# Two-layer cross-attention on one core: the last third of the even entries' queries one filling point later, and layer 2's image-key copy on ScalarE in place of GpSimd

## The chip, the cores and the metric

The kernel runs on one core of a Trainium2 chip. TensorE (PE) multiplies matrices into the eight banks of PSUM. VectorE (DVE), ScalarE (ACT) and GpSimd (POOL) do the elementwise work, and SyncE (SP) issues nearly all DMA transfers. Each engine works through its own instructions in order and waits on semaphores for the others. The metric is the device time of one execution in microseconds (us), and the time of a kernel is the median of its runs.

## The reference

Sixteen entries (B) of 256 rows and 320 channels pass through two cross-attention layers with 20 heads of 16 channels. The context of an entry has 256 rows of 512 channels. In layer 1 its first 77 rows (`T0`) are text and the others image tokens; in layer 2 the first 252 (`T1`) are text and the last 4 image tokens. Layer 1 in short:

```python
q = hidden_states @ Wq
k_text, v_text = text @ Wk, text @ Wv
probs = softmax(q_h @ k_h.T * scale)                 # per head, over the text
text_out = probs @ v_h
scores = q_h @ ip_k_h.T * scale                      # ip_k = ip @ Wk_ip
sem = (softmax(q @ k_text.T * scale) @ text) @ ip.T * scale
ip_probs = softmax(scores + 0.5 * sem) * spatial_mask
hs = text_out + ip_probs @ ip_v_h
out = hs @ Wout + bout + residual
```

Layer 2 does the same on layer 1's output with its own weights, but takes the semantic term per head, from that head's own text probabilities, and with both sides scaled to length one:

```python
qsem = l2norm(probs_t @ text_ehs)                    # per head
sem = qsem @ l2norm(ip_ehs).T
probs_ip = softmax(q @ k_ip.T * scale + 0.5 * sem) * spatial_mask
```

## The kernel before

**Slots.** The work is cut into 160 slots: 80 for layer 1, 16 entries by 5 groups of four heads, and then 80 for layer 2. In slot k of layer 1 (`slot0`), PE transposes the row maxima of slot k+1 (`maxima0`, line 708), computes scores for slot k+2 (`score0`, 701), multiplies for the exponentials of slot k (`turned0`, 723) and multiplies the probabilities of slot k-1 by the values (`attend0`, line 766). ACT copies the transposed maxima out of PSUM (line 710, tile `mt`) and issues their transfer into the query tiles `qs` (711); it also takes the exponentials (726). POOL multiplies them by the semantic factors (729), and DVE takes the row maxima (702, 703). Slots of layer 2 (`slot1`) have the exponentials at line 879, the maxima's transpose at 884, copy at 886 and transfer at 887, and the semantic products on all engines (894 rounds the probabilities on ACT, 895 takes the remainder on POOL, 904 multiplies on PE, 905 multiplies on DVE).

**Filling.** Between those steps, at three points of each slot, `fill(now)` runs whatever other work is due: keys, queries, values, semantics, the closing projections. Each such task is a generator with a list of due times in slots. PE's instructions stand in the order in which the code issues them. Those of the other four engines are ordered by a scheduler, so an edit of one task may move instructions on them too.

**Queries.** `queries0(b)` loads an entry's rows (`xq`), splits them in a high and a low half (`hq`) and projects in three pieces: two of eight matmuls (line 567) and a third of five (line 570, m = 2). The third is emptied by `evacuate` in four steps: ACT copies at 266 (`q`) and 267 (`both`), DVE works at 268 and 269, and then SP writes the third piece to DRAM (`qd<-q`), from where the slots' tiles `qs` are loaded four slots ahead. The output projection of an earlier entry (`close0`) uses the same two lines with the split rows `ho`, which ACT makes at 554 and 555 and POOL at 556 and 557. All these products share the rotating PSUM banks named `X`.

**Keys of layer 2.** `keys1(b)` does the same for the keys, in three pieces with the two buffers `kst` in turn. The last four columns of each piece (`T1:`) are the image tokens' keys, which were computed for all entries at once in `kip`. Line 490 copies them into `kst`, high and low part at once, and `keys_out` writes `kst` to DRAM (`kd<-kst`, two transfers per piece, at line 84). The copy must wait until the transfers of the piece that used that buffer before have read it.

Of the kernel before, what the change touches and what calls it, by code (L numbers as in the profile page):

```python
# [26 lines left out]
T1 = S - NIP  # L27
# [23 lines left out]
def xattn2(  # L51
# [27 lines left out]
    nc = tc.nc  # L79
    f = lambda ap: ap.bitcast(F32)  # L80
# [10 lines left out]
    def bank(tag="X"):  # L91
        return ps.tile([128, 512], F32, tag=tag, name=tag, bufs=BANKS[tag])
# [18 lines left out]
    def buf(tag, shape, dtype=F32, bufs=1, name=None):  # L111
        if tag in ("wB", "wD", "vr", "raw"):
            return sb.tile(shape, dtype, tag=tag, name=name or tag, bufs=bufs)
        size = 1
        for d in shape[1:]:
            size *= d
        if tag not in slots:
            slots[tag] = [0, dtype] + [const_tile([128, max(size, words.get(tag, 0))], f"{tag}_{i}", dtype) for i in range(bufs)]
        n, kind, *ring = slots[tag]
        assert kind == dtype and len(ring) == bufs, tag  # L120
        slots[tag][0] += 1
        t = ring[n % bufs][: shape[0], :size]
        names = "abcd"[: len(shape) - 1]
        if len(names) > 1:
            t = t.rearrange(f"p ({' '.join(names)}) -> p {' '.join(names)}", **dict(zip(names, shape[1:])))
        return t

    def const_tile(shape, tag, dtype=F32):
        return const.tile(shape, dtype, tag=tag, name=tag)
# [121 lines left out]
    def prod_m(out, w, m, rhs, kt):  # L251

        if m < 2:
            prod(out, lambda s, k: w(s, k, m), rhs, kt)
            return out
        for i in range(2 * kt):
            mm(out, w(0, i // 2, 2), rhs(i % 2, i // 2), start=i == 0, stop=i == 2 * kt - 1)  # L257
        return out

    def evacuate(hi, lo, out, m):  # L260

        if m < 2:
            return halves(hi, lo, out)
        hi, lo = hi[:64], lo[:64]
        both = buf("both", list(hi.shape), bufs=2)
        nc.scalar.copy(hi, out[:64])
        nc.scalar.copy(both, out[64:])
        nc.vector.tensor_sub(out[:64], out[:64], f(hi))
        nc.vector.tensor_add(lo, out[:64], both)  # L269

    def context(b, n, wait=0):

        tiles, parts = [], []
        for k in range(0, 4, 3 - n):
            src = cT_d[:, b * S : (b + n) * S].rearrange("(k p) t -> p k t", p=128)[:, k : k + 3 - n]
            ct = buf("cta" if n == 1 or k < 2 else "ctb", [128, 2, 512], FR, bufs=SIZES["CTA" if n == 1 or k < 2 else "CTB"], name="ct")
            split = lambda t: t.rearrange("p (k t) -> p k t", t=n * S)
            parts.append((src, split(ct[:, 0]), split(ct[:, 1])))
            tiles.append(ct)
        yield from in_turn(parts, wait, "rawc raw" if n == 2 else "rawc", nc.gpsimd if wait and b != 2 else nc.vector)  # L280
        if n == 2:
            return lambda s, k: tiles[k][:, s].rearrange("p (b t) -> p b t", b=2)
        return lambda s, k: tiles[k // 2][:, s, (k % 2) * S : (k % 2 + 1) * S]
# [25 lines left out]
    kip = const_tile([128, 2, 3, BI], "kip", FR)  # L309


    def keys_out(d, m, kst, b=slice(None)):

        rows = slice(m * 128, min(m * 128 + 128, CH))
        n = rows.stop - rows.start
        for r, s in ((slice(0, 2), 0), (slice(2, 3), 1)):
            src = kst[:n, s, b].rearrange("p b t -> p (b t)").unsqueeze(1)
            dma(d[r, rows, b].rearrange("r p b t -> p r (b t)"), src.to_broadcast([n, r.stop - r.start, src.shape[2]]))
# [163 lines left out]
    def keys1(b):  # L482
        ct = ct1[b] = yield from context(b, 1, 0.3)
        for m in range(3):
            kst = buf("kst", [128, 2, 2, S], FR, bufs=SIZES["KST"]).rearrange("p s b t -> p (s b t)")
            kst = kst[:, : 2 * S].rearrange("p (s b t) -> p s b t", s=2, b=1)
            kp = prod_m(bank()[:, :T1], w1["k"], m, lambda s, k: ct(s, k)[:, :T1], 4)
            n = 64 if m == 2 else 128
            evacuate(kst[:, 0, 0, :T1], kst[:, 1, 0, :T1], kp, m)
            nc.gpsimd.tensor_copy(kst[:n, :, 0, T1:], f(kip[:n, :, m, 4 * b : 4 * b + 4]))  # L490
            keys_out(kd[1][b], m, kst)
            if m < 2:
                yield
        wv = w1["wv"]
        two = [buf("tph", [128, 2, S], FR, bufs=2, name="two") for i in range(2)]
        twice = doubled[b] = lambda k: two[k // 2][:, k % 2, :T1]
        for k in range(4):
            nc.gpsimd.tensor_copy(wv[:, :, k, H * D :], f(ct(slice(None), k)[:, :, T1:]))
        for k in range(4):
            nc.scalar.activation(twice(k), f(ct(1, k)[:, :T1]), AF.Copy, scale=2.0)  # L500
        yield
# [48 lines left out]
    def split(src, neg, eng, tag):  # L550

        hl = buf(tag, [128, 5, S], FR)
        order = queued if tag == "hq" else lambda inst: inst
        order(nc.scalar.copy(hl[:, 0:2], src[:, 0:2]))
        order(nc.scalar.activation(hl[:, 2], src[:, 2], AF.Copy, scale=neg))
        order(eng.tensor_sub(hl[:, 3:5], src[:, 0:2], f(hl[:, 0:2])))
        order(eng.tensor_add(hl[:, 2], src[:, 2], f(hl[:, 2])))
        return hl
# [15 lines left out]
    def queries(l, a):  # L574
        qh = buf("q", [128, 2, 3, S], FR)

        def evac(m, pp):
            evacuate(qh[:, 0, m], qh[:, 1, m], pp, m)

        qd = dram.tile([3, CH, S], F32, tag=f"qd{l}", name=f"qd{l}", bufs=2)  # L580
        steps = project(l, wq[l], a, evac)
        for m in range(2):
            next(steps)
            yield
        for r, s in ((0, 0), (1, 1), (2, 0)):
            dma(qd[r, :256].rearrange("(m p) t -> p m t", p=128), qh[:, s, :2])
        next(steps)
        for r, s in ((slice(0, 3, 2), 0), (slice(1, 2), 1)):
            to = qd[r, 256:].rearrange("r p t -> p r t")
            dma(to, qh[:64, s, 2].unsqueeze(1).to_broadcast(list(to.shape)))  # L590
        yield
        return qh, qd
# [4 lines left out]
    def load(src, tag):  # L597
        x = buf(tag, [128, 3, S])
        dma(x, src.rearrange("(k p) t -> p k t", p=128))
        return x  # L600

    def queries0(b):
        x = early.pop(b) if b in early else load(xT_d[b], "xq")
        yield
        xs = split(x, tmask[:, 5:6], nc.gpsimd, "hq")
        yield
        return (yield from queries(0, xs))
# [662 lines left out]
    def task(key, times, make, *needs):  # L1270
        tasks[key] = [times, 0, make, needs, len(tasks)]
# [38 lines left out]
    def shifted(n, *times):  # L1310

        return [RAMP(n + t) for t in times]
# [4 lines left out]
    for c in range(B // 2):  # L1317
        n, k = 10 * c, [("k0", c)] if c else []
        if c:
            task(("k0", c), FIRST["k0"] if c == 1 else shifted(n, -14.4, -13.3, -13, -12.4, -12, -11.4, -10.8, -9.8, -9.4, -9, -8.4), lambda c=c: keys0(c),  # L1320
                 *([("w4", 0)] if c > 1 else []))
            task(("q0", 2 * c), shifted(n, -11.8, -11, -10, -9, -8), lambda b=2 * c: queries0(b))
        task(("q0", 2 * c + 1), shifted(n, -4.4, -4, -3, -2.8, -2), lambda b=2 * c + 1: queries0(b))
        if c:
            task(("m0t", 2 * c), shifted(n, -7.4), lambda b=2 * c: tokens0(b), *k)
        task(("m0t", 2 * c + 1), shifted(n, -4.8), lambda b=2 * c + 1: tokens0(b), *k)
        task(("v0", 2 * c), shifted(n, -7, -5.4, -5), lambda b=2 * c: values0_(b), *k)
        task(("v0", 2 * c + 1), shifted(n, -4, -3.8, -3.4), lambda b=2 * c + 1: values0_(b), *k)
        for b, t in ((2 * c, (-7.4, -6.4, -6, -5.4, -5, -4.4, -3.4)), (2 * c + 1, (-2.4, -1.8, -1.4, -1, -0.8, 0, 1.2))):
            if b:  # L1330
                task(("s0", b), FIRST["s0"] if b == 1 else shifted(n, *t), lambda b=b: semantic0(b), ("q0", b), ("m0t", b))
            task(("c0", b), shifted(5 * b, *((6, 7.6, 8, 8.2) if b % 2 == 0 else (6, 7.2, 8.2, 9.2) if b < B - 1 else (7, 7.67, 8, 8.67))), lambda b=b: close0(b), ("gathered", 0, b), ("w4", 0))
    for b in range(B):
        n = NS + 5 * b
# [340 lines left out]
```

## Time and profile before

| | |
|---|---|
| median of 3 runs | 1478.3 us (1476.85 to 1479.2) |
| profiled execution | 1483.24 us |
| its span on the core | 1481.5 us |
| mean granted clock of PE | 0.983 |
| busy: PE, POOL, DVE, ACT | 1418.0, 1217.7, 1133.5, 897.5 us |
| line 490 on POOL | 48 copies, 192 ns each in the middle |

The profile is one execution, in microseconds from the start of its span. A row of the timeline gives the start, the length, the engine, the line and the operation with its tiles, and in brackets how long the engine had stood idle before it and what released it. A row of the table of waits gives the total, the number and the longest. Layer 1's slots run to about 640 us and layer 2's from about 690, where an entry of five slots takes 48.9 us.

### The profile page before, as it was taken

Reading aid. Unit: us, or ns where it says so; the run is one execution under the profiler, and the core shown is the slowest. Engines: PE = TensorE matmul, PEld = TensorE weight load, DVE = VectorE, ACT = ScalarE, POOL = GpSimd, SP = SyncE. Lnnn points to the kernel's source line nnn. Section 1 sums busy time; section 2 is a strip of 40 time slices with the busy share of each in tenths; the row PEclk is TensorE's granted clock in tenths of the full one; section 3 lists DMA queues with packets and bytes.
Section 4 is the critical chain, followed back from the end, with each engine's and each line's share of the span. In section 5 each row is a group of like instructions: output and inputs, shape, how many; then the busy total and the mean of one; then the engine's idle time right before and its main releaser. Section 6 shows DMA issues by size and latency. Waiting matters only on the chain.

```text
span 1481.5 us, 35836 instructions
## 1 busy us (share of the span) xinstructions
PE 1418.0 (96%) x12578; PEld 1147.1 (77%) x12578; DVE 1133.5 (77%) x2527; ACT 897.5 (61%) x2173; POOL 1217.7 (82%) x1590
## 2 busy tenths in 40 slices
PE   8889999999999989789999999999999999999998
PEld 7778888888888878567778777877787777777765
DVE  6567777777777788867878888788878878887886
ACT  6346565656565645546666676666766766676663
POOL 6259898989999978889678888788878888888885
PEclk8899999999999999989999999999999999999999
DMA  7766777776777665765444444444444444533401
GB/s 241 199 205 202 214 209 214 204 213 193 229 205 219 201 202 160 198 201 157 138 105 124 126 135 110 125 140 120 116 119 138 121 116 120 147 114 93 125 25 51
DMA packets 229118, 232.43 MB, mean 157 GB/s; under 512 B 38186, under 2 KB 198860, under 8 KB 228940
## 3 DMA queue, kind: packets, MB, share of 16 engines
q1 hardware_dynamic: 226736, 229.18, 54.2%
q8 instruction: 100, 1.64, 0.5%
q10 hardware_dynamic: 2204, 0.97, 0.3%
q14 instruction: 78, 0.64, 0.1%
HBM read 117.65 MB, written 77.07 MB: 131 GB/s over the span
## 4 chain that ended last, share of the span: by engine, by line
PE 69%; POOL 10%; DVE 9%; DMA 4%; ACT 3%; issue 3%; SPq 1%; ACTq 0%; DVEq 0%; POOLq 0%
PE X L904 14%; PE X L247 14%; PE P L766 6%; PE X L567 6%; PE S L701 5%; PE P L916 4%; PE P L926 4%; PE T L723 4%; POOL wt L895 3%; PE T L859 3%; PE S L865 3%; POOL P L729 3%; PE X L257 2%; DMA qs<-qd 2%; PE X L570 1%
## 5 line engine op out<-in xcount | busy, mean ns | idle before, releaser
L729 POOL TENSOR_TENSOR P<-P,rs 128x512 f32<-128x512 f32 x320 | 408.1, 1304 | 80.4 <-ACT P L726 79.7
L895 POOL TENSOR_TENSOR wt<-P,ctb 128x512 f32<-128x512 f32 x316 | 402.4, 1293 | 39.8 <-ACT ctb L894 39.3
L904 PE MATMUL X<-ctb,gm 128*128 128x512 f32 x1106 | 295.4, 400 | 4.5 <-DVE wt L905 4.5
L726 ACT ACTIVATE P<-T 128x512 f32<-128x512 f32 x320 | 175.8, 594 | 178.7 <-PE T L723 135.3
L905 DVE TENSOR_TENSOR wt<-X,wt 128x512 f32<-128x512 f32 x320 | 217.3, 683 | 35.8 <-PE X L904 28.0
L904 PEld LDWEIGHTS X<-ctb,gm 128*128 128x128 f32 x1106 | 194.1, 189 | 39.1 <-DVE wt L905 7.9
L879 ACT ACTIVATE P<-T 128x512 f32<-128x512 f32 x320 | 173.2, 593 | 79.6 <-PE T L859 76.6
L894 ACT ACTIVATE ctb<-P 128x512 fp32r<-128x512 f32 x316 | 182.4, 626 | 14.9 <-PE X L904 13.6
L867 DVE TENSOR_REDUCE mn<-S 128x4 fp32r<-128x1008 f32 x160 | 191.2, 1195 | 0.0
L703 DVE TENSOR_REDUCE mn<-S 128x4 fp32r<-128x716 f32 x160 | 142.6, 891 | 0.0
L766 PE MATMUL P<-P,vr 128*32 128x256 f32 x1920 | 128.6, 390 | 2.7 <-POOL P L729 1.9
L701 PE MATMUL S<-ks,qs 125*128 125x256 f32 x640 | 118.1, 308 | 10.2 <-DVE mn L703 4.7
L701 PEld LDWEIGHTS S<-ks,qs 125*128 125x128 f32 x640 | 88.9, 195 | 46.9 <-issue 28.1
L723 PE MATMUL T<-qs,ks 127*128 127x256 f32 x640 | 106.0, 289 | 0.2 <-ACT P L726 0.2
L777 DVE STREAM_TRANSPOSE nt<-P 128x512 f32<-128x512 f32 x80 | 57.2, 715 | 52.2 <-PE P L766 51.3
L702 DVE TENSOR_REDUCE mn<-S 128x4 fp32r<-128x308 f32 x160 | 74.4, 465 | 28.5 <-PE S L701 28.2
L766 PEld LDWEIGHTS P<-P,vr 128*32 128x32 f32 x1920 | 56.2, 111 | 47.3 <-POOL P L729 7.7
L723 PEld LDWEIGHTS T<-qs,ks 127*128 127x128 f32 x640 | 90.6, 195 | 1.1 <-ACT P L726 0.6
L926 PE MATMUL P<-wt,zone 128*32 128x256 f32 x1280 | 85.3, 379 | 0.7 <-DVE wt L905 0.7
L916 PE MATMUL P<-P,v1t 128*32 128x256 f32 x1280 | 85.9, 385 | 0.0
L247 PE MATMUL X<-wC,cta 128*128 128x324 f32 (+1 forms) x480 | 79.9, 313 | 0.3 <-DVE kst L269 0.3
L865 PE MATMUL S<-ks,qs 48*128 48x256 f32 x640 | 74.5, 309 | 3.9 <-DVE mn L867 2.5
(389 smaller groups left out, 2999.3 us busy)
## 6 DMA issues: line engine op xcount, KB each, us to landing
qd<-q SPq DMA_DIRECT2D x96, 256.0 KB
qs<-tph SPq DMA_DIRECT2D x64, 308.0 KB
qs<-qd SPq DMA_DIRECT2D x80, 192.0 KB
ks<-kd SPq DMA_DIRECT2D x80, 192.0 KB
ks<-kd SPq DMA_DIRECT2D x160, 96.0 KB
qs<-qd SPq DMA_DIRECT2D x160, 96.0 KB
kd<-kst SPq DMA_DIRECT2D x57, 256.0 KB
ks<-M SPq DMA_DIRECT2D x64, 215.4 KB
```

The lines of the kernel that those rows point to most:

```text
L247: last = mm(out, lhs(a, k), rhs(b, k), start=i == 0, stop=i == len(terms) - 1)
L701: mm(sp[:, h], Q[: XROW + T0, h, t * 128 : (t + 1) * 128], K[: XROW + T0, h], start=True, stop=True)
L723: mm(st[p][:, j], K[:KS0, 2 * p + j, t * 128 : (t + 1) * 128], Q[:KS0, 2 * p + j], start=True, stop=True)
L726: exp = anchor(nc.scalar.activation(pt, st[p], AF.Exp, scale=SCALE))
L729: anchor(nc.gpsimd.tensor_mul(pt, pt, rs[:, t : t + 1].to_broadcast([128, 2, S])))
L766: mm(pv[32 * s : 32 * s + 32, o : o + S], v[:, vt, h : h + 32], P[k, s // 2][:, t, s % 2], start=vt < 2, stop=vt != 1,)
L867: anchor(nc.vector.tensor_reduce(mn[:, :, t], sp[:, :, :T1], axis=AX.X, op=ALU.max))
L879: anchor(nc.scalar.activation(P[k, u][:, t], st[u], AF.Exp, scale=SCALE))
L894: nc.scalar.activation(R[k, u][:, t], P[k, u][:, t], AF.Copy, scale=0.5)
L895: anchor(nc.gpsimd.tensor_sub(W[k, u][:, t], P[k, u][:, t], f(R[k, u][:, t])))
L904: mm(yp, gm[:, gb], R[k, u][:, kt], start=i == 0, stop=i == len(blocks[n]) - 1)
L905: w1["wt"] = nc.vector.tensor_mul(W[k, u][:, n], yp, W[k, u][:, n])
```

## The change

One due time and one engine differ:

```diff
@@ keys1 @@
             evacuate(kst[:, 0, 0, :T1], kst[:, 1, 0, :T1], kp, m)
-            nc.gpsimd.tensor_copy(kst[:n, :, 0, T1:], f(kip[:n, :, m, 4 * b : 4 * b + 4]))
+            nc.scalar.copy(kst[:n, :, 0, T1:], f(kip[:n, :, m, 4 * b : 4 * b + 4]))
             keys_out(kd[1][b], m, kst)
@@ tasks @@
-            task(("q0", 2 * c), shifted(n, -11.8, -11, -10, -9, -8), lambda b=2 * c: queries0(b))
+            task(("q0", 2 * c), shifted(n, -11.8, -11, -10, -9, -7.8), lambda b=2 * c: queries0(b))
```

The second edit moves the third piece of entry 2c's queries from the last filling point of slot 10c - 9 to the first of slot 10c - 8, for c = 2 to 7; for c = 1 the order stays as it was. On PE this is what it does at c = 2 (`X_1934` of before and `X_1919` of after are the transposed maxima, `hq` the queries' input, `ho` the closing projection's):

```order
 L257 MATMUL X_1904<-ctb_1_80,wB_86 128x360 x2
-L570 MATMUL X_1922<-hq_0_254,wE_0_82 128x256 x5
-L708 MATMUL X_1934<-ident_r_75,mn_1_544 16x128
+L708 MATMUL X_1919<-ident_r_75,mn_1_544 16x128
 L701 MATMUL S_66<-ks2_96,qs2_92 128x256 x4
 L723 MATMUL T_67<-qs0_90,ks0_94 128x256 x2
 L723 MATMUL T_68<-qs0_90,ks0_94 128x256 x2
-L567 MATMUL X_1952<-ho_0_184,wF_0_998 128x256 x8
+L567 MATMUL X_1937<-ho_0_184,wF_0_998 128x256 x8
+L570 MATMUL X_1950<-hq_0_254,wE_0_82 128x256 x5
 L766 MATMUL P_69<-P_2_124,vr_99 32x256 x2
```

L570 now follows L567 and stands directly ahead of line 766. With one bank less in use before it, L567 no longer takes the bank that the transposed maxima had in the same stretch; L570 does.

The first edit puts the 48 copies into ACT's order. At layer 2's first entry (690 to 696 us of the profile before) ACT's order changes so (`P` are exponentials of `T`, `ctb` their rounding):

```order
 L158 CAST kst_0_182<-X_8672 128x252
 L879 ACTIVATE P_0_122<-T_8691 128x512
+L490 CAST kst_1_183<-kip_106 64x2x4
 L879 ACTIVATE P_1_123<-T_8692 128x512
 L894 ACTIVATE ctb_0_79<-P_0_122 128x512
 L894 ACTIVATE ctb_1_80<-P_1_123 128x512
+L490 CAST kst_0_182<-kip_106 128x2x4
 L879 ACTIVATE P_0_122<-T_8723 128x512
 L879 ACTIVATE P_1_123<-T_8724 128x512
```

Two copies now stand ahead of three of the four exponentials. In a later entry (the one at 1327 us) the copy for the next entry's first piece stands between two pairs of exponentials on ACT, in after:

```order
L158 CAST kst_1_183<-X_16483 128x252
L879 ACTIVATE P_2_124<-T_16502 128x512
L879 ACTIVATE P_3_125<-T_16503 128x512
L490 CAST kst_1_183<-kip_106 128x2x4
L879 ACTIVATE P_2_124<-T_16538 128x512
L879 ACTIVATE P_3_125<-T_16539 128x512
L886 CAST mt_0_598<-X_16552 8x128
```

Before, the same rows stood there without the L490. The scheduler's order differs in small ways elsewhere, mostly on POOL and DVE around the six places of the second edit: POOL's L557 moves ahead of two multiplications of line 729 at c = 3 and behind two of them and L785 at c = 5.

## The prediction

> **What bounds the kernel now.** I read the page's busy times first, then the chain of work that ended last, then the table of waits of the whole span, and at last the timelines of the places that the change touches. Page, parts 1 and 4:
>
> ```profile
> PE 1418.0 (96%) x12578; PEld 1147.1 (77%) x12578; DVE 1133.5 (77%) x2527; ACT 897.5 (61%) x2173; POOL 1217.7 (82%) x1590
> PE 69%; POOL 10%; DVE 9%; DMA 4%; ACT 3%; issue 3%; SPq 1%; ACTq 0%; DVEq 0%; POOLq 0%
> ```
>
> TensorE (PE) is busy 96% of the span, so an edit of other engines counts only where PE stands still. Waits of PE (total us, times, longest), and the group of line 490:
>
> ```profile
> PE X L567 <- ACT mt L710: 4.6, 6, 0.8
> PE X L904 <- DVE wt L905: 4.5, 14, 2.0
> PE S L701 <- DMA qs<-qd: 1.7, 3, 0.8
> PE X L567 <- POOL ho L557: 0.8, 1, 0.8
> L490 POOL CAST kst<-kip x48: 182/192/477, 558.6 to 1372.0; 128x8 fp32r<-128x8 f32 x32, 64x8 fp32r<-64x8 f32 x16
>   DMA kd<-kst: 14.0, 9
> ```
>
> The first line is what edit 1 aims at: 4.6 us, at exactly its six places (c = 2 to 7). Edit 2 takes 48 copies of 0.192 us, 9.2 us in all, from GpSimd (POOL). No PE row names them, but nine times POOL stood before such a copy, 14.0 us together, until an earlier kd<-kst transfer had left the buffer. Those waits change engine with the copy.
>
> The profiled execution took 1483.24 us (span 1481.5 and 1.74 around it), 4.9 above the median 1478.3 of the runs. I sum against the profile and carry the sum to the median. About 0.2%, 3 us, is what a measurement can tell from no change.
>
> **Edit 1: the queries' last five matmuls.** Place c = 2, and the two rows that matter at c = 4 (POOL's L557 and PE's L766):
>
> ```profile
> 160.48 0.75 PE L570 MATMUL X<-hq,wE 128*128 128x256 f32 x5
> 161.06 0.22 PE L708 MATMUL X<-ident_r,mn 128*16 128x128 f32 x1
> 163.13 1.31 PE L567 MATMUL X<-ho,wF 128*128 128x256 f32 x8 [0.84 <-ACT mt L710]
> 163.15 0.73 POOL L557 TENSOR_TENSOR ho<-hT,ho 128x256 fp32r<-128x256 f32 x1
> 164.37 1.50 PE L766 MATMUL P<-P,vr 128*32 128x256 f32 x24
> 312.33 0.73 POOL L557 TENSOR_TENSOR ho<-hT,ho 128x256 fp32r<-128x256 f32 x1
> 313.90 1.50 PE L766 MATMUL P<-P,vr 128*32 128x256 f32 x24
> ```
>
> L567 (the output projection of entry b-2) waits 0.84 us because its PSUM bank was that of the row maxima's transpose, which ScalarE (ACT) empties only after the queries' two copies. With L570 behind L567 the bank is free, and this wait goes. What is late next: the last two of L567's eight matmuls read what POOL's L557 writes, and it ends at 163.88, 0.49 before L766 starts. L557 stands behind four multiplications and one L785 that POOL does without a pause, so it does not come earlier because PE does. Then two matmuls (0.49 with the first's latency) and the moved L570 (161.06 less 160.48, 0.58) follow, where before only the two did: L766 starts 0.58 later. L570's own wait, for ACT's L710, lies under this.
>
> By place: c = 2, 6 and 7 (at 7 the POOL wait of 0.8 stands in the table) +0.58 each. c = 4: L557 ends at 313.06, so L766 at 313.06 + 0.49 + 0.58 = 314.13, +0.23. c = 5: before, L557 stood ahead of two of the multiplications, now it stands behind all four as at c = 2; a wait of 0.4 goes and that gate comes, +0.5. c = 3 is the other way round: L557 moves ahead of two multiplications and holds nothing any more. Freed altogether a place gains 0.84 and the 0.31 by which L567's stretch to L766 (163.13 to 164.37, 1.24) exceeds eight matmuls at L570's pace (8 x 0.58 / 5 = 0.93): -1.15. The two multiplications that are now late can take some of it, so between -1.15 and +0.58 I take -0.9, nearer to the end that the freed bank gives. Sum 3 x 0.58 + 0.23 + 0.5 - 0.9 = **+1.6 us**; bounds +3.5 (0.58 at all six) and -6.4 (L557 nowhere in the way: -1.15 at five places, -0.6 at c = 5).
>
> What else moves: ACT's L710, two exponentials and the L711 transfer go ahead of the queries' copies (earlier by 0.75), DVE's L268/L269 and SP's qd<-q of the last third come some 1.6 us later, behind kd<-kst. I cost that at nothing: the qs<-qd loads are made four slots of work ahead. If that cover is gone, the 1.7 us of PE waiting for qs<-qd is what grows.
>
> **Edit 2, at the change of layers.** POOL's longest wait of the nine is 5.36 us before 656.03, with line 729's multiplications queued behind it, whose first exponential is done about 654.7:
>
> ```profile
> 654.09 1.09 ACT L726 ACTIVATE P<-T 128x512 f32<-128x512 f32 x2 [1.55 <-DMA ks<-kd]
> 656.03 0.18 POOL L490 CAST kst<-kip 64x8 fp32r<-64x8 f32 x1 [5.36 <-DMA kd<-kst]
> 657.42 0.84 POOL L991 TENSOR_TENSOR M<-M,kb 128x384 fp32r<-128x384 f32 x1
> 663.39 0.63 PE L766 MATMUL P<-P,vr 128*32 128x256 f32 x4 [0.60 <-POOL P L729]
> 692.05 0.62 PE L766 MATMUL P<-P,vr 128*32 128x256 f32 x4 [0.38 <-POOL P L729]
> ```
>
> From there POOL's timeline has no gap until about 700, and PE waits for it at 663.39 and 692.05. Without the copy POOL starts 1.3 earlier, but its next instruction needs the M<-vipd transfer, issued behind the one waited for; I take 0.7 of the 1.3, and 2 x 0.15 for two further copies that leave the row: **-1.0 us** (bounds -1.6 and -0.2).
>
> **Edit 2, at layer 2's first entry.** ACT is in order, so what waits in front of its exponentials delays them:
>
> ```profile
> 692.86 0.19 POOL L490 CAST kst<-kip 64x8 fp32r<-64x8 f32 x1
> 695.49 0.20 POOL L490 CAST kst<-kip 128x8 fp32r<-128x8 f32 x1
> 693.14 1.09 ACT L879 ACTIVATE P<-T 128x512 f32<-128x512 f32 x2 [0.73 <-PE T L859]
> 694.11 0.23 ACT L886 CAST mt<-X 8x128 fp32r<-8x128 f32 x1
> 696.22 0.50 PE L859 MATMUL T<-qs,ks 49*128 49x256 f32 x4 [0.49 <-DMA qs<-mt]
> 698.02 0.99 PE L859 MATMUL T<-qs,ks 49*128 49x256 f32 x4 [0.30 <-ACT P L879]
> 691.64 1.33 SPq L84 DMA_DIRECT2D kd<-kst x2
> ```
>
> Now one copy stands between the two exponentials of the pair before these rows, and the next ahead of the pair of 693.14. POOL made them unwaited at 692.86 and 695.49, so their transfers had landed by then; the second's were issued from 691.64 to 692.97. If it lands at about 694.9 (the small mt transfer of these rows took 1.9 from L886's end to PE's start, which gives 692.97 + 1.9; the bound is later), ACT's copy (0.24, as ACT's L886) ends at 695.14 and the pair starts 2.0 late. L886 follows, then its transfer, for which PE waits at 696.22 already: the wait is on the path, and ACT's row of work up to the exponentials behind the 698.02 wait is too. **+2.0 us** (bounds +0.5, two copies without a wait, and +2.6, the landing at 695.49).
>
> **Edit 2, in the other fourteen entries.** Per entry three copies: behind the third piece's hi rounding, where ACT was idle anyway; between the two pairs of L879; ahead of the pair at the end. Here POOL waited eight times, and the end of its wait is the landing. Three are harmless: two in the entry at 736 to 744, where PE stands still for other reasons and ACT is idle, one at 1134.06, well ahead of PE's need. The first and the last of four alike of the second kind (the others ended at 890.40 and 1232.67), and one of the third kind:
>
> ```profile
> 792.70 0.19 POOL L490 CAST kst<-kip 128x8 fp32r<-128x8 f32 x1 [0.91 <-DMA kd<-kst]
> 793.44 0.76 PE L570 MATMUL X<-hq,wE 128*128 128x256 f32 x5
> 1326.22 0.44 SPq L84 DMA_DIRECT2D kd<-kst  x1
> 1327.57 1.09 ACT L879 ACTIVATE P<-T 128x512 f32<-128x512 f32 x2 [1.21 <-PE T L859]
> 1330.50 0.19 POOL L490 CAST kst<-kip 128x8 fp32r<-128x8 f32 x1 [0.96 <-DMA kd<-kst]
> 1331.31 0.76 PE L570 MATMUL X<-hq,wE 128*128 128x256 f32 x5
> 847.80 0.19 POOL L490 CAST kst<-kip 128x8 fp32r<-128x8 f32 x1 [0.43 <-DMA kd<-kst]
> 847.98 1.14 PE L904 MATMUL X<-ctb,gm 128*128 128x512 f32 x4
> ```
>
> The pair that ran at 1327.57 would start at 1330.50 + 0.24 and end 1.09 later, 1331.83. PE's L570 writes the bank which that pair reads, and started at 1331.31: +0.52. At 792.70: 794.03 against 793.44, +0.59; the two between give +0.41 and +0.44. At 847.80 the first exponential of its pair ends near 848.64, and L904 needs its bank at 847.98: +0.65. Sum **+2.6 us**. In the entries where POOL did not wait the landing is at least a microsecond earlier than L570 needs, so nothing there. Bounds: 0 (no late landing) and +6 (0.45 in each of fourteen). The 9.2 us taken from POOL itself buy nothing: POOL is idle 18% of the span, and the PE wait on DVE's L905 (0.2 an entry, beside one of 2.0) falls where no such copy is.
>
> One page bears on this term. The Trainium skill, "DMA: Bandwidth & Descriptors", section "Anatomy of one DMA", gives a DMA a fixed cost of about 2.0 us plus its bytes at 436 GB/s. By it this 128 KB transfer, issued at 1326.22 to 1326.66, lands near 1329.0 (estimate), PE's bank is free in time, and the term is 0. The trace has 1330.50, 3.8 after the issue, so it does not agree, and I keep 2.6.
>
> **Sum:** +1.6 - 1.0 + 2.0 + 2.6 = +5.2 us: 1488.4 for a profiled execution, 1478.3 + 5.2 = **1483.5 us** for the median, slower by 0.35%.
>
> **Rivals.**
> *The waits on ACT do not reach PE* (no change). The two layer-2 terms rest on landing times to half a microsecond. If transfers land 0.6 sooner, the +2.6 is 0, and if the second copy of the first entry waits for nothing, little of the +2.0 is left; against it, five such waits of POOL in fourteen entries. 1478.3 + 1.6 - 1.0 + 0.5 = 1479.4.
>
> *The freed bank is worth what it looks* (faster). If L557 is done about 1.2 us sooner, PE gains at all six places. For it: before, PE's first stop is ACT, not POOL, at each of them. Against it: 163.88 plus two matmuls is 164.37, just where L766 starts. It decides from L557 ending before about 162.7 at c = 2. -6.4 - 1.0 + 4.6 = -2.8: 1475.5.
>
> *The clock falls at the first entry* (slower still). After some idle stretches the granted clock drops:
>
> ```profile
> 741.33 0.50 PE L865 MATMUL S<-ks,qs 48*128 48x256 f32 x4 [2.51 <-DVE mn L867]
> 741.30:745.20 3.90, 3.87 (x18) 3.38 (x19) 3.11 (x7) 1.01 (x3) 0.63 (x3) 0.59 0.45 152
> 610.67 0.34 PE L642 MATMUL X<-ident,sp 128*77 128x128 f32 x1 [2.66 <-ACT sp L638]
> 610.70:614.70 4.00, 4.00 (x58) 3.34 (x58) 2.20 (x5) 2.37 (x6) 2.54 (x5) 1.00 0.47 137
> ```
>
> After 2.51 us of idling PE ran 3.9 us at 0.59 (the figure after the five busy times), which costs 3.9 x 0.41 = 1.6; after 2.66 it kept 1.00. My new gap at 696 is 0.49 + 2.0 = 2.5, so it may go either way: 1483.5 + 1.6 = 1485.1. The Trainium skill, "TensorE: Matmul & The Clock Gate", section "HAM oscillation", says that gaps above about 3.4 us are what re-throttles. By it a gap of 2.5 costs no clock; the drop after 2.51 differs, and leaves this case a chance.
>
> **How the numbers follow.** Forecast 0.40, its clock case 0.12: slower 0.52. Waits that do not reach PE 0.28: same. The freed bank 0.20: faster. Low end 1474.0, the faster rival with the waits on ACT a third smaller; high end 1489, the clock case with landings late in most of the entries. The forecast's own range, with its terms at their nearer bounds, is 1480 to 1487.
>
> **What would show it.** Right: L567 without an ACT wait but with one for POOL's L557, at c = 2, 6 and 7; no POOL wait before 656; a new ACT wait for kd<-kst before L879 near 694 and PE's wait for qs<-mt there of about 2.5; some `PE X L570 <- ACT P L879` of 0.4 to 0.6 in layer 2. Wrong: L766 of layer 1 earlier than in the rows above, ACT copies that hardly wait, or layer 2 entries of the old length throughout.

## The result and the profile after

The changed kernel took 1495.06 us in the median of four runs (1491.89 to 1500.56), and the kernel before, in as many runs, 1478.75 (1476.85 to 1481.74). The ratio is 1.0111 [1.0081, 1.014]: 16.3 us slower, where 5.2 were predicted and 1489.0 was the upper end. The profiled execution of after took 1492.98 us (span 1490.9). It lies 2.1 below its kernel's median and that of before 4.5 above its own, so the two traces differ by 9.4 us of span where the medians differ by 16.3. The accounts below explain the 9.4.

Busy times and the shares of the chain that ended last, from the page of after:

```profile
PE 1420.4 (95%) x12578; PEld 1143.8 (77%) x12578; DVE 1130.1 (76%) x2527; ACT 900.7 (60%) x2221; POOL 1208.9 (81%) x1542
PE 61%; DVE 11%; POOL 10%; DMA 7%; ACT 4%; issue 3%; SPq 2%; ACTq 0%; DVEq 0%; POOLq 0%
```

No engine does noticeably more work. PE's share of the chain falls from 69% to 61%, DVE's rises from 9% to 11%, and that of the transfers from 4% to 7%: more of the chain runs by DVE and transfers. The table of waits of after (engine, tile and line that waits, what released it: total us, times, longest) and the group of line 490 say for which:

```profile
ACT kst L490 <- DMA kd<-kst: 87.2, 44, 4.2
DVE X L268 <- ACT both L267: 30.1, 42, 2.8
PE X L567 <- POOL ho L557: 6.8, 5, 1.5
PE S L865 <- DVE mn L867: 4.7, 8, 0.8
PE T L859 <- DMA qs<-mt: 1.8, 1, 1.8
PE X L570 <- ACT P L879: 1.1, 4, 0.3
PE X L904 <- ACT P L879: 1.0, 2, 0.7
```

```profile
L490 ACT CAST kst<-kip x48: 180/198/203, 558.3 to 1381.6; 128x8 fp32r<-128x8 f32 x32, 64x8 fp32r<-64x8 f32 x16
  DMA kd<-kst: 87.2, 44
```

On POOL, 9 of the 48 copies waited for their buffer, 14.0 us together. On ACT 44 of them do, 87.2 us. Two other waits grew with it, that of DVE's line 268 for ACT and that of PE's line 865 for DVE's row maxima (in before a single one, the 2.51 us at 741.33). In before they were:

```profile
DVE X L268 <- ACT both L267: 13.8, 31, 1.2
PE S L865 <- DVE mn L867: 2.5, 1, 2.5
```

**Layer 1.** PE in after at c = 2, and its L766 at c = 3:

```profile
161.04 0.50 PE L567 MATMUL X<-ho,wF 128*128 128x256 f32 x2 [1.53 <-POOL ho L557]
161.39 0.74 PE L570 MATMUL X<-hq,wE 128*128 128x256 f32 x5
162.06 1.50 PE L766 MATMUL P<-P,vr 128*32 128x256 f32 x24
235.12 1.50 PE L766 MATMUL P<-P,vr 128*32 128x256 f32 x24
```

The wait on ACT's L710 is gone at all six places. At c = 2 one of 1.53 for POOL's L557 stands there instead, and the moved L570 follows; the table above has five such waits, 6.8 us. At c = 3 there is no wait. I lined the PE rows of the two traces up one to one. At 120 us of before, ahead of every changed instruction, after runs 2.8 us early, which is the spread between executions. At 520 us it is 2.8 early still: the first five places lose 1.4 together, and three waits for `qs<-qd` that came out shorter or longer give 1.0 back. The sixth place gains 0.8. At 650 us after is 2.5 early.

**The change of layers.** PE's longest stop there is before L701, for DVE's row maxima; in before, and behind it in after:

```profile
654.16 1.22 PE L701 MATMUL S<-ks,qs 125*128 125x256 f32 x4 [3.48 <-DVE mn L703]
650.28 0.74 PE L701 MATMUL S<-ks,qs 125*128 125x256 f32 x4 [2.16 <-DVE mn L703]
```

At 692 us of before, after is 3.6 early, 1.1 more than at 650. POOL no longer stands 5.36 us for its copy, and its multiplication L729 begins 0.7 us behind this L701 in place of 2.0. But then POOL waits 1.17 us at L991 for `M<-vipd`, and PE's three waits for POOL's L729 add up to 1.76 us, against 1.55 in before. The gain is the 1.32 us by which the stop before L701 is shorter, and that stop is not POOL's: it is 2.28 us in e1 below, where the copies stay on POOL, and 3.12 in e2, where they are on ACT.

**Layer 2's first entry.** Rows of ACT and PE in after:

```profile
688.32 0.20 ACT L490 CAST kst<-kip 64x8 fp32r<-64x8 f32 x1 [0.90 <-DMA kd<-kst]
690.81 0.20 ACT L490 CAST kst<-kip 128x8 fp32r<-128x8 f32 x1 [0.76 <-DMA kd<-kst]
693.86 0.50 PE L859 MATMUL T<-qs,ks 49*128 49x256 f32 x4 [1.75 <-DMA qs<-mt]
695.78 1.28 PE L859 MATMUL T<-qs,ks 49*128 49x256 f32 x4 [0.43 <-ACT P L879]
```

Both copies wait, and PE's wait for `qs<-mt` grows from 0.49 to 1.75. What follows shows in the windows (start:end, length, then busy times of PE, its weight loads, DVE, ACT and POOL, the granted clock, the DMA share and GB/s), that of after first and that of before behind it:

```profile
696.00:702.00 6.00, 6.00 (x23) 5.18 (x24) 3.17 (x8) 1.93 (x6) 2.05 (x3) 0.50 0.52 134
```

```profile
698.00:708.00 10.00, 9.87 (x79) 8.17 (x83) 6.90 (x16) 6.39 (x13) 7.90 (x10) 1.00 0.54 143
```

For 6 us the granted clock is 0.50. In before it stayed at 1.00. By PE's rows the slow stretch costs 2.6 us.

**A later entry.** The same stretch as in the prediction at 792.70, in after, ACT, DVE and PE in order of time:

```profile
790.56 0.20 ACT L490 CAST kst<-kip 128x8 fp32r<-128x8 f32 x1 [4.15 <-DMA kd<-kst]
790.66 1.08 ACT L879 ACTIVATE P<-T 128x512 f32<-128x512 f32 x2
791.79 0.87 PE L570 MATMUL X<-hq,wE 128*128 128x256 f32 x5 [0.29 <-ACT P L879]
792.45 0.36 ACT L266 CAST kst<-X 64x252 fp32r<-64x252 f32 x1 [0.59 <-ACT mt L886]
793.24 0.42 DVE L268 TENSOR_TENSOR X<-X,kst 64x252 f32<-64x252 f32 x1 [1.92 <-ACT both L267]
796.82 1.19 DVE L867 TENSOR_REDUCE mn<-S 128x4 fp32r<-128x1008 f32 x1
798.16 0.51 PE L865 MATMUL S<-ks,qs 48*128 48x256 f32 x4 [0.66 <-DVE mn L867]
```

The copy stops ACT for 4.15 us. Two exponentials are late, and PE's L570 waits for them; that was predicted. But behind them in ACT's queue stand the two copies (266, 267) which empty the third piece of this entry's keys. DVE stands idle 1.92 us for them at L268, then does its queue in order, and the row maxima L867 that end it come late. L865 needs the bank of scores which L867 reads, and waits 0.66. Seven entries have such a gap at L865. POOL is delayed too: its waits for ACT's L894 grow from 39.3 us to 69.9 over the whole span. That goes no further. Between 764 and 1412 us of before, no wait of PE in the tables of either trace is put down to POOL, and DVE's waits for POOL are about as long in after as in before.

### The profile page after: what moved, and what is told of

It is laid out like the page before. It is cut to its first block, busy times and chain, and to the rows that moved or that the text cites. A ratio compares the mean times of both kernels' runs of the same rounds, so it can differ in the third digit from the quotient of the medians.

```text
span 1490.9 us, 35821 instructions
## 1 busy us (share of the span) xinstructions
PE 1420.4 (95%) x12578; PEld 1143.8 (77%) x12578; DVE 1130.1 (76%) x2527; ACT 900.7 (60%) x2221; POOL 1208.9 (81%) x1542
## 4 chain that ended last, share of the span: by engine, by line
PE 61%; DVE 11%; POOL 10%; DMA 7%; ACT 4%; issue 3%; SPq 2%; ACTq 0%; DVEq 0%; POOLq 0%
PE X L904 13%; PE X L247 12%; PE P L766 6%; PE X L567 5%; PE S L701 4%; POOL P L729 4%; PE P L916 3%; PE T L723 3%; PE P L926 3%; PE S L865 3%; POOL wt L895 3%; DMA kd<-kst 2%; PE T L859 2%; SPq L84 2%; DVE mn L867 2%
## 5 line engine op out<-in xcount | busy, mean ns | idle before, releaser
L729 POOL TENSOR_TENSOR P<-P,rs 128x512 f32<-128x512 f32 x320 | 408.2, 1303 | 83.2 <-ACT P L726 82.3
L895 POOL TENSOR_TENSOR wt<-P,ctb 128x512 f32<-128x512 f32 x316 | 401.7, 1291 | 71.9 <-ACT ctb L894 69.9
L904 PE MATMUL X<-ctb,gm 128*128 128x512 f32 x1106 | 295.4, 400 | 5.0 <-DVE wt L905 3.9
L905 DVE TENSOR_TENSOR wt<-X,wt 128x512 f32<-128x512 f32 x320 | 217.0, 682 | 34.9 <-PE X L904 32.0
L904 PEld LDWEIGHTS X<-ctb,gm 128*128 128x128 f32 x1106 | 194.1, 189 | 40.0 <-DVE wt L905 7.2
L879 ACT ACTIVATE P<-T 128x512 f32<-128x512 f32 x320 | 171.9, 594 | 43.8 <-PE T L859 40.6
L867 DVE TENSOR_REDUCE mn<-S 128x4 fp32r<-128x1008 f32 x160 | 191.1, 1194 | 0.0
L894 ACT ACTIVATE ctb<-P 128x512 fp32r<-128x512 f32 x316 | 182.4, 625 | 14.4 <-PE X L904 13.1
L766 PE MATMUL P<-P,vr 128*32 128x256 f32 x1920 | 130.8, 396 | 4.4 <-DVE tmp L783 2.2
L701 PE MATMUL S<-ks,qs 125*128 125x256 f32 x640 | 116.4, 304 | 7.7 <-DMA ks<-M 2.4
L701 PEld LDWEIGHTS S<-ks,qs 125*128 125x128 f32 x640 | 87.6, 192 | 45.4 <-issue 27.2
L766 PEld LDWEIGHTS P<-P,vr 128*32 128x32 f32 x1920 | 56.8, 112 | 49.5 <-POOL P L729 7.4
L865 PE MATMUL S<-ks,qs 48*128 48x256 f32 x640 | 76.0, 313 | 6.2 <-DVE mn L867 4.7
```

The source lines that it names most:

```text
L701: mm(sp[:, h], Q[: XROW + T0, h, t * 128 : (t + 1) * 128], K[: XROW + T0, h], start=True, stop=True)
L729: anchor(nc.gpsimd.tensor_mul(pt, pt, rs[:, t : t + 1].to_broadcast([128, 2, S])))
L766: mm(pv[32 * s : 32 * s + 32, o : o + S], v[:, vt, h : h + 32], P[k, s // 2][:, t, s % 2], start=vt < 2, stop=vt != 1,)
L867: anchor(nc.vector.tensor_reduce(mn[:, :, t], sp[:, :, :T1], axis=AX.X, op=ALU.max))
L879: anchor(nc.scalar.activation(P[k, u][:, t], st[u], AF.Exp, scale=SCALE))
L894: nc.scalar.activation(R[k, u][:, t], P[k, u][:, t], AF.Copy, scale=0.5)
```

## The experiments

Two theories. **W**: the copy's wait for its buffer, at the head of ACT's in-order queue, delays what stands behind it. **O**: the wait is harmless, and the copies' own time and their place among ACT's other work cost the time. Within W, **D** says that the delay reaches PE mainly by DVE (L267, L268, L867, L865) and not by the exponentials of L879. Every ratio is to the kernel before on the same chip, with its 95% interval. The waits come from each kernel's profiled execution.

**Each half of the change by itself.** e1 has the prediction's edit 1, the queries, and e2 its edit 2, the copy ("The change" above counts the two the other way round):

```diff
-            task(("q0", 2 * c), shifted(n, -11.8, -11, -10, -9, -8), lambda b=2 * c: queries0(b))
+            task(("q0", 2 * c), shifted(n, -11.8, -11, -10, -9, -7.8), lambda b=2 * c: queries0(b))
```

> Only the later third of the queries; the copy stays on GpSimd. Theory W (the loss comes from ScalarE's waits for kd<-kst in front of its exponentials): nothing of the loss is here, between -1 and +2.5 us against before; at the six places line 766 moves by +0.5 or so, and by -1.1 at c = 3. Rival Q (the move of the queries is what costs, through L557 on GpSimd or through the shifted order of the other engines): +6 us or more.

```diff
-            nc.gpsimd.tensor_copy(kst[:n, :, 0, T1:], f(kip[:n, :, m, 4 * b : 4 * b + 4]))
+            nc.scalar.copy(kst[:n, :, 0, T1:], f(kip[:n, :, m, 4 * b : 4 * b + 4]))
```

> Only the copy on ScalarE; the queries stay. Theory W: nearly the whole loss, +9 to +16 us, with ScalarE waiting some 80 us in all for kd<-kst before line 490 and TensorE waiting for DVE's L867 and ScalarE's L879 in layer 2. Rival Q: under +5 us.

e1 took 1479.57 us against 1480.97, 1.0003 [0.9988, 1.0017]. e2 took 1494.34, 1.0091 [1.0067, 1.0114]. A wait of e1 and two of e2:

```profile
PE X L567 <- POOL ho L557: 7.2, 5, 1.5
```

```profile
ACT kst L490 <- DMA kd<-kst: 88.5, 44, 4.2
PE S L865 <- DVE mn L867: 3.7, 7, 0.7
```

The queries' edit trades 4.6 us of waiting on ACT for 7.2 on POOL and changes the time by nothing that can be measured. The loss is the copy's.

**Four places in place of two.** If the copy finds a free place, it need not wait. The two buffers are cut in halves that are used in turn, with the copy on ACT (e3) and on POOL (e4):

```diff
-            kst = buf("kst", [128, 2, 2, S], FR, bufs=SIZES["KST"]).rearrange("p s b t -> p (s b t)")
-            kst = kst[:, : 2 * S].rearrange("p (s b t) -> p s b t", s=2, b=1)
+            half = (3 * b + m) % 2
+            if half == 0 or "kst" not in w1:
+                w1["kst"] = buf("kst", [128, 2, 2, S], FR, bufs=SIZES["KST"]).rearrange("p s b t -> p (s b t)")
+            kst = w1["kst"][:, 2 * S * half : 2 * S * half + 2 * S].rearrange("p (s b t) -> p s b t", s=2, b=1)
```

> The copy on ScalarE as in e2, but layer 2's kst pieces use the two halves of each buffer in turn, four places in place of two, so that the transfers of the piece before in the same place have landed long before the copy. The same 48 copies on ScalarE. Theory W: the waits of line 490 fall from some 80 us to under 10 and the time is within 3 us of before. Rival O (the 48 copies as such, 0.2 us each on ScalarE, or the changed order of its row, cost the time): as slow as e2, +9 us or more.

> The copy on GpSimd as before, with the four places. Takes away GpSimd's 14 us of waiting before line 490 and nothing else. Theory W: -3 to +1 us, since in before only the wait that ends at 656 us stands on a path that TensorE follows. Rival P (GpSimd's waits at 736 to 744 and in later entries cost TensorE too): -5 us or more.

e3 took 1494.91, 1.0095 [1.0072, 1.0118], e4 1478.49, 0.9978 [0.996, 0.9995]. But e3's copy (its line 492) still waits:

```profile
ACT kst L492 <- DMA kd<-kst: 85.1, 42, 4.2
```

The copies at 785.49, 792.89 and 799.78 us of e3 wait until the transfers issued at 782.64, 788.97 and 797.70 have landed, each time those of the piece directly before. Why the copy into a free half is held for them was not found out. The edit did not take the wait away, and e3 tells nothing between W and O. Why e4 gains 0.2% stays open: its POOL copies wait 15.6 us, about as long as before.

**The copy behind the piece's own emptying.** The wait can be avoided without a buffer. In e5 the copy stays on ACT, but is ordered behind ACT's copy of its own piece out of PSUM (line 158, or 267 for the third piece), which comes later; e6 does the same with the copy on POOL:

```diff
-        order(nc.scalar.copy(hi, src))
+        anchors["hi"] = order(nc.scalar.copy(hi, src))
...
-        nc.scalar.copy(both, out[64:])
+        anchors["hi"] = nc.scalar.copy(both, out[64:])
...
-            nc.gpsimd.tensor_copy(kst[:n, :, 0, T1:], f(kip[:n, :, m, 4 * b : 4 * b + 4]))
+            queued(nc.scalar.copy(kst[:n, :, 0, T1:], f(kip[:n, :, m, 4 * b : 4 * b + 4])), anchors["hi"])
```

> All 48 copies on ScalarE, but each ordered behind its own piece's last PSUM copy on ScalarE (line 158 or 267), which writes the same buffer and so has waited for the same transfers already. Same copies, same engine, no early wait. Theory W (the waits in front of the exponentials cost the time): line 490 waits under 5 us in all, TensorE's waits for DVE's L867 and ScalarE's L879 in layer 2 are gone, and the time is between -4 and +3 us of before. Rival O (48 copies of 0.2 us on ScalarE, or a row that holds them at all): +9 us or more, as e2.

> The copies stay on GpSimd, ordered behind their own piece's last copy on ScalarE in the same way, so that GpSimd no longer waits for a transfer in front of its multiplications. Theory W: line 490's 14 us of waiting fall under 4, and the time is -4 to 0 us. Rival P' (GpSimd's early copies were free, and late ones hold its subtractions of line 895 up): 0 to +4 us.

e5 took 1474.14 us against 1477.54: 0.9973 [0.9953, 0.9994]. e6 took 1475.66: 0.9992 [0.997, 1.0014]. The group of line 490 in e5 (busy, mean ns, idle time before it), two of its waits, and the later entry:

```profile
L490 ACT CAST kst<-kip 128x8 fp32r<-128x8 f32 (+1 forms) x48 | 9.6, 200 | 0.0
```

```profile
DVE X L268 <- ACT both L267: 12.4, 28, 1.3
PE S L865 <- DVE mn L867: 0.4, 1, 0.4
```

```profile
781.88 0.37 ACT L267 COPY both<-X 64x252 f32<-64x252 f32 x1
782.81 0.41 DVE L268 TENSOR_TENSOR X<-X,kst 64x252 f32<-64x252 f32 x1
786.25 1.19 DVE L867 TENSOR_REDUCE mn<-S 128x4 fp32r<-128x1008 f32 x1
788.14 0.40 PE L865 MATMUL S<-ks,qs 48*128 48x256 f32 x4
```

ACT does the same 48 copies, 9.6 us, and never waits for one. In this entry L268 starts without waiting, L865 too, and the whole loss is gone. O falls as far as the copies' own time goes: 48 copies on ACT cost nothing that can be measured when they do not wait. Their place in ACT's row changed together with the wait, so e5 does not part these two; but a copy that did not wait would hold up what stands behind it by its own 0.2 us only. This version is also faster than both kernels, by 3.4 us than before. Its interval overlaps e6's, so whether ACT is the better engine for the copy is not settled.

**Which copy.** Only the first (e7), second (e8) or third (e12) piece's copies go to ACT; shown for e7:

```diff
-            nc.gpsimd.tensor_copy(kst[:n, :, 0, T1:], f(kip[:n, :, m, 4 * b : 4 * b + 4]))
+            (nc.scalar.copy if m == 0 else nc.gpsimd.tensor_copy)(kst[:n, :, 0, T1:], f(kip[:n, :, m, 4 * b : 4 * b + 4]))
```

> Only the first pieces' copies (m = 0, sixteen of 48) on ScalarE: in layer 2 those that stand between the two pairs of L879. Theory W, by where the trace of after loses time against before: these carry the waits of L570 (about 2 us), of L865 on DVE's L867 (about 6) and of DVE's L905 (about 2), so +6 to +11 us. If the loss were spread evenly over the 48, +4 to +5.

> Only the second pieces' copies (m = 1, sixteen of 48) on ScalarE: in layer 2 those ahead of the last pairs of L879 of an entry. Theory W: they carry only the waits of L904 on ScalarE's L879 (1.6 us in all), so 0 to +3 us. If the loss were spread evenly over the 48, +4 to +5.

> Only the third pieces' copies (m = 2) on ScalarE: in layer 2 those ahead of line 554, where ScalarE was idle for 1.6 us. Theory W: nothing, -3 to +2 us; of the entry at 690 only its first copy is here. If the loss were spread evenly, +4 to +5.

e7 took 1492.5 us: 1.0092 [1.0063, 1.012]. e8 took 1480.84: 1.0003 [0.9975, 1.0031]. e12 took 1481.35: 1.0014 [0.9996, 1.0033]. The copies of the first pieces, a third of the 48, cost as much as all 48 in e2. The waits of ACT's L490 and of DVE's L268 in e7, and behind them those of e8 and of e12:

```profile
ACT kst L490 <- DMA kd<-kst: 40.4, 15, 4.2
DVE X L268 <- ACT both L267: 26.6, 39, 2.6
PE S L865 <- DVE mn L867: 5.5, 6, 2.4
```

```profile
ACT kst L490 <- DMA kd<-kst: 17.3, 8, 6.1
DVE X L268 <- ACT both L267: 12.2, 31, 0.8
```

```profile
ACT kst L490 <- DMA kd<-kst: 22.8, 15, 2.2
DVE X L268 <- ACT both L267: 13.5, 32, 1.1
```

The medians leave up to 0.3% open for e8 and e12. PE's rows are sharper, because they leave out what differs between executions ahead of the later entries. Lined up one to one with those of before, over the stretch from 764 to 1412 us of before, PE loses in one execution of each:

| kernels | ACT's waits for `kd<-kst` before its copies, us | DVE's L268 for ACT's L267, us | lost from 764 to 1412, us |
|---|---|---|---|
| after, e2, e3 (48 copies on ACT) | 87.2, 88.5, 85.1 | 30.1, 27.4, 27.3 | 12.7, 14.2, 12.5 |
| e7 (first pieces) | 40.4 | 26.6 | 11.3 |
| e8 (second), e12 (third) | 17.3, 22.8 | 12.2, 13.5 | 1.7, 0.0 |
| e5, e11 (48 behind their own piece) | none | 12.4, 14.5 | -0.7, -0.7 |
| e1, e4, e6 (copies on POOL) | none | 13.9, 12.2, 12.8 | 1.2, 0.0, -0.5 |

ACT waits in e8 and e12 as well (in e8 another 12.2 us before L490, for which the profile shows no releaser), and that costs next to nothing. The loss goes with DVE's row: 12 to 15 us of waiting where at most 1.7 us are lost, 27 to 30 where 11 to 14 us are. As the rows above show, it depends on where the copies stand: the next entry's first piece is placed as soon as its buffer is handed out, ahead of the third piece's L266 and L267 of the present entry.

**Is it DVE's row that carries the delay?** In e9 DVE itself empties the third pieces, so that no DVE instruction there waits for ACT's L267; the copies are on POOL. e10 is e9 with the first pieces' copies on ACT, as in e7:

```diff
-        nc.scalar.copy(hi, out[:64])
-        nc.scalar.copy(both, out[64:])
+        nc.vector.tensor_copy(hi, out[:64])
+        nc.vector.tensor_copy(both, out[64:])
```

> Base for e10: before, but the third pieces' two copies out of PSUM (lines 266 and 267, of keys and queries in both layers) are made by DVE in place of ScalarE, so that DVE's L268 no longer stands behind ScalarE. DVE does four more instructions of 0.35 us an entry and layer. No theory differs here: -4 to +6 us against before.

> e9 and the first pieces' copies on ScalarE as in e7. Theory D (most of the loss goes by DVE: ScalarE late, so L267 late, so DVE's in-order L268 late, so the row maxima of L867 behind it late, so TensorE's L865 waits for their bank): that link is cut, and e10 is only 2 to 6 us above e9, with hardly a wait of L865 for L867. Rival B (the loss goes by the PSUM banks that the late exponentials free, and by GpSimd behind L894): e10 is 9 us or more above e9.

e9 took 1499.57 us: 1.0139 [1.0109, 1.0169], far above what was expected. e10 took 1503.76: 1.0185 [1.0158, 1.0213]. A page line and a wait of e9, and behind them two waits of e10:

```profile
PE 1423.0 (95%) x12578; PEld 1149.4 (77%) x12578; DVE 1176.0 (78%) x2657; ACT 857.4 (57%) x2043; POOL 1217.8 (81%) x1590
```

```profile
PE S L865 <- DVE mn L867: 8.4, 15, 2.7
```

```profile
ACT kst L490 <- DMA kd<-kst: 42.6, 15, 4.1
PE S L865 <- DVE mn L867: 6.7, 13, 1.6
```

I had taken DVE's idle 23% for room. Here it is not: 42.5 us more of work on DVE cost 22 us. L865 waits for the maxima 15 times, but only 8.4 us in all; where the rest goes I did not trace. On this base the first pieces' copies on ACT wait as long as in e7 (42.6 us). The medians of e10 and e9 differ by 4.2 us, where e7 lost 15.0. Six and five runs, each spread over more than 11 us, do not settle that: the means differ by 6.1, give or take 7. PE's rows say more. Between 764 and 1412 us e10 loses 3.1 us against e9, where e7 loses 11.3 against before. This speaks for D, since with ACT's L267 out of DVE's way most of the loss is gone, and the 3.1 left is near the 3.6 which the waits for the exponentials cost in after. It is not proof. The base is itself held up by DVE, which may hide part of the loss, and L865 still waits 13 times for L867, where hardly a wait was expected.

**The good copy with the queries' edit.** e11 is e5 with the due time of e1:

> e5 with the queries' third piece later: both edits of the change, with the copy behind its own piece's PSUM copy. Theory W: as e5, -5 to +1 us against before, and the queries' move adds nothing (between -1 and +2.5 us against e5).

e11 took 1475.51 us, 0.9991 [0.9976, 1.0007], with five waits of L567 for POOL in it, 7.8 us. So the queries' edit adds nothing to the better kernel either.

**Where the better kernel gains.** Between 712 and 770 us of before, PE's rows gain 3.7 us in e5, 3.5 in e6 and 4.0 in e11. Rows of before, and behind them one of e5:

```profile
736.63 3.03 DVE L161 TENSOR_TENSOR wF<-rawc,wF 128x256 fp32r<-128x256 f32 x2 [1.38 <-ACT wF L158]
737.07 2.50 POOL L895 TENSOR_TENSOR wt<-P,ctb 128x512 f32<-128x512 f32 x2
728.58 0.56 DVE L161 TENSOR_TENSOR wF<-rawc,wF 128x256 fp32r<-128x256 f32 x2 [1.77 <-ACT wF L158]
```

In before POOL's copy waits 1.85 us until 736.63, and its two multiplications then run beside the second of DVE's two L161. That one takes 2.68 of the 3.03 us, and the stop of 2.51 before PE's L865 at 741.33 follows from it. In every kernel in which POOL waits for its copy at this place the same instruction is long (2.68 us in before, e1, e7 and e9, 1.30 in e4, e8 and e10). In the other seven it takes 0.22, and PE stops 0.9 us at most. So e5's gain of 3.4 us over before is of the size of this place. That it is this place is not settled: e12 gains 3.2 us there in its trace and nothing in its median. Why DVE is slow beside POOL was not tested.

## Why the prediction was wrong, by its steps

- **Edit 1, +1.6 us: right in kind.** The mechanism is the one told: the wait for ACT's L710 is replaced by one for POOL's L557. Measured from row to row, c = 2 lost 0.58 (0.58 predicted) and c = 3 gained 1.1 (0.9). c = 4 and 5 lost 0.7 and 1.1, more than predicted (0.23 and 0.5), and c = 6 lost 0.2. c = 7 gained 0.8 where 0.58 was to be lost: it had waits for both ACT and POOL before (0.84 and 0.80) and has one of 1.06. The six places together lost 0.5. The rival of the freed bank, -6.4, is refuted by e1.
- **Change of layers, -1.0 us: the number came out, by luck.** After gained 1.1 there, and the 5.36 us wait of POOL is gone. But PE's waits for POOL, by which the gain was to come, did not shrink (1.55 and 1.76 us). What shrank is a stop for DVE's row maxima, which is as short in e1, without the copy's move.
- **First entry, +2.0 us: right in kind, and its rival came with it.** The two copies waited 0.90 and 0.76 on ACT. PE's waits grew by 1.26 and 0.13, less than the 2.0 taken, but the clock then fell to 0.50 for 6 us, which cost 2.6 where the rival allowed 1.6. From 692 to 710 after lost 4.0. It got 3.0 back by 764: L865's stop of 2.51 in before is 0.84 in after, and no fall of the clock follows it. The prediction had called POOL's waits at 736 to 744 harmless, since PE stood still there "for other reasons". The rows above put that stop down to the first of them.
- **The other fourteen entries, +2.6 us: the step that failed.** Between 764 and 1412 us after lost 12.7, five times the term. The four waits of L570 came in the four entries that were named, for about 2.0 us against 1.96 predicted; L904's waits for the exponentials cost 1.6, not 0.65. Some 5.8 us came where L865 stops for DVE's row maxima, to which the prediction gave nothing (PE's rows shift by 0.5 to 1.0 at each of the seven, more than the gaps alone), 1.7 at L904 and L526 behind DVE's L905, and the rest in small pieces. The landing 3.8 us after the issue, which the prediction sets against the section "Anatomy of one DMA" of the Trainium skill, "DMA: Bandwidth & Descriptors", is no clean test of it: that section is headed for the GpSimd path, and these transfers are issued by SyncE, two to a piece.
- **Why that step failed.** It asked of each late copy only which of PE's banks the next exponentials hold: "In the entries where POOL did not wait the landing is at least a microsecond earlier than L570 needs, so nothing there." L570 was the wrong need. The copy is placed where its buffer is handed out, up to 4.2 us ahead of the landing (2.7 on average for the first pieces, in e7), and behind it stand not only two exponentials but also L266 and L267, on which DVE, in order too, waits with its row maxima behind. POOL's nine waits in before were no count of ACT's: POOL came to most copies after the landing, being late itself, and ACT comes to 44 of 48 ahead of it. The upper bound of +6 did allow a late copy in all fourteen entries, but at L570's price of 0.45 each, where the stretch cost about 0.9 an entry. That the first pieces' copies, waiting on ACT, cause the loss is shown by e2, e5 and e7. That it travels mostly by DVE is read from the rows and supported by e7, e8, e12 and e10; no run isolates it.
- **The rival in which the waits do not reach PE** is refuted by e2.

What was lost: -2.8 at the start, +0.3 from 120 to 650, -1.1 at the change of layers, +4.0 and -3.0 at the first entry, +12.7 after it, -0.6 in the closing stretch. That is 9.5 by PE's rows; the spans differ by 9.4. The other 7 of the 16.3 between the medians lie in which executions were profiled.

## What to carry to other kernels

When work moves to another in-order engine, its waits move with it and are new there: read for each moved instruction when its operand or buffer comes free, and follow the whole queue behind it, through the second engine, to PE. A wait's place says more than its size: 23 us of waiting cost nothing in the rows of e12, while 40 us in e7 cost 11. A cheap instruction whose only dependence is the reuse of a buffer should be ordered behind something that its own piece needs anyway; one such anchor turned +0.9% (e2) into -0.3% (e5).

## What the runs showed of the hardware

- The granted clock fell to 0.50 for 6 us after a stop of PE of 1.75 us and one of 0.43 (at 693.86 and 695.78 of after); after 0.84 at 740.07 it stayed at 1.00. In before it fell after 2.51 and not after 2.66. One place of the program shows both: PE's L708 stops 2.68 us in before (until 531.50) and 2.61 in after (until 528.65), and in the windows behind it, before first, the clock is 1.00 and 0.50. The length of one stop does not tell which.

```profile
531.50:535.50 4.00, 3.98 (x41) 2.79 (x41) 1.97 (x5) 1.33 (x5) 0.54 (x2) 1.00 1.00 350
528.65:532.65 4.00, 4.00 (x25) 3.24 (x29) 1.99 (x5) 1.34 (x5) 0.53 (x2) 0.50 1.00 353
```

- Late landings recur: the four entries whose `kd<-kst` transfers ended late in before are the four in which L570 waits in after. In e2 and e7 it waits in three of the same four. So they seem to belong to the order of the program and not to chance.
- The same program's executions spread by up to 16 us (the kernel before, 33 runs on the chip of e5: 1469.63 to 1485.64), so a difference of 0.3% took 12 runs against 33.
